# A sparse four-layer graph network on one core: two columns share one sum in the scan, and the first table is planned ahead of most of it

## The chip, the core and the metric

The kernel runs on one core of one Trainium2 chip. A core has five engines with instruction streams of their own: PE (TensorE, matmuls into PSUM), DVE (VectorE), ACT (ScalarE), POOL (GpSimd, which here issues the indirect DMAs) and SP (SyncE, which issues the plain DMAs). They meet at semaphores; transfers run on 16 DMA engines. The metric is the device time of one run in microseconds, less is better. The time before is 2148.46 us, the median of three runs (2143.64 to 2156.99).

## What is computed

Node features `x` (4096 x 256) go through four graph attention layers, each behind a layer norm, a ReLU and a residual. `adj` (4096 x 4096, int32) is 0 or 1, symmetric, with ones on the diagonal, and about 9 ones in a row.

```python
_a = jax.random.bernoulli(jax.random.fold_in(_gk, 2), 0.000976562, (4096, 4096))
_a = jnp.logical_or(_a, jnp.swapaxes(_a, -1, -2))
_a = jnp.logical_or(_a, jnp.eye(4096, dtype=bool))
adj = _a.astype(jnp.int32)
...
def _L0_gnn_ref(h, adj, W, a):
    Wh = (h @ W).reshape(n, heads, d)
    s_i = jnp.einsum('nhd,hd->nh', Wh, a[:, :d])
    s_j = jnp.einsum('nhd,hd->nh', Wh, a[:, d:])
    e = jax.nn.leaky_relu(s_i[:, None, :] + s_j[None, :, :], negative_slope=0.2)
    e = jnp.where((adj == 0)[:, :, None], -jnp.inf, e)
    alpha = jax.nn.softmax(e, axis=1)
    out = jnp.einsum('ijh,jhd->ihd', alpha, Wh).reshape(n, heads * d)
    return jax.nn.elu(out)
...
h = jnp.maximum(_layernorm(x, axis=-1), 0.0)
x = x + _L0_gnn_ref(h, adj, L0_gnn_W, L0_gnn_a)
```

Layers 1 to 3 have the same form with other score functions. Since a row has few neighbours, the kernel turns `adj` into lists of column numbers once and gathers only the neighbours' rows in every layer.

## The kernel before

The rows are 32 blocks of 128 ("rows" below: block r). The program has a first stage that makes the lists (`lists`, `scan`), then a re-reading of all rows in the order of their degrees (`reload`), the rest of layer 0 (`late`), layers 1 to 3 (`layer`), and a verdict. If a condition that the lists rely on does not hold (too many neighbours, for example), the verdict is bad and a dense version of the whole network runs behind it. Only the first stage is changed.

**The scan.** For every row block, four quarters of `adj` (128 x 1024 int32) come by DMA into eight buffers (`load`, L265) and ACT turns them into fp8 (`cast`, L276), which also sums the edges. `marks` (L491 to L498) handles 512 columns: one matmul multiplies the 0/1 columns with a diagonal matrix of MARK = 8192, a small one adds another MARK at the node's own column (so that it comes out first), and one adds each column's place, n minus its number. A PSUM value over 8192 is then an edge and says which; two MAX8 take the 8 largest of each 256 columns. Eight calls make a row block: 16 MAX8. `merge` (L506, L508) takes the 24 largest of these 128 candidates with three MAX8 and two replacements, and `number` (L514, L515, on ACT) turns them into column numbers.

**The table.** Beside it, for two row blocks at a time (`table`, u = 0 to 15), ACT applies norm and ReLU (L340), PE transposes (L348), ACT copies (L351), PE multiplies with the layer's weights (L892, fp32), and ACT copies the products to `s_keep` (L356); SP writes four row blocks at a time to a table in DRAM (L399). DVE's statistics for the norm are L580 and L581, its roots are L586 to L596.

**Early gathers.** `early(j)` handles row blocks 2j and 2j + 1: POOL fetches 6 neighbours of each of the 256 nodes with 12 indirect DMAs (L899, tile `s_g`, three buffers), DVE makes scores (L534 to L542), ACT the exponentials (L546), DVE the sums and the node's own term (L548, L550) and two multiplications of the gathered rows by their shares (L558, one per row block), PE adds the seven terms in fp32 (L564, L567), ACT copies the result (L571).

**Placing.** `sort` counts the degrees and finds each node's place (L607 to L650); `to_place` scatters a row block to that place with one indirect DMA (L656, 32 in all). `reload` waits for all of them.

**What sets the order.** PE, DVE, ACT and SP run in the order in which the program records the work. It is written by hand: a loop over steps `at` (four per 2048 columns, 256 in all for the scan) emits what `plan(engine, at, ...)` put there. In a step, ACT's and PE's planned work comes ahead of that step's marks, DVE's and POOL's behind them. Before, early gather j is fetched from step max(4(10 + j), 16(j + 1) + 3) on; its seven PE matmuls stand at every second step, the first on gathered rows four steps after the second multiplication; `sort` is planned 28 steps before the scan's end, and 12 of the 32 scatters may go out before it ends.

Of the kernel before, what the change touches and what calls it, by code (L numbers as in the profile page):

```python
# [9 lines left out]
F32 = mybir.dt.float32  # L10
# [38 lines left out]
MARK = 8192.0  # L49
# [30 lines left out]
class Sparse:  # L80
# [155 lines left out]
    def lists(self, w0, a0):  # L236
        tc, nc, nt, n = self.tc, self.nc, self.nt, self.n
        self.ok = self.const.tile([P, 8], F32, name="s_ok")
        nc.vector.memset(self.ok, 1.0)
        with ExitStack() as ctx:  # L240
            self.pool = ctx.enter_context(tc.tile_pool(name="s_scan", bufs=2))
            self.pacc = ctx.enter_context(tc.tile_pool(name="s_macc", bufs=4, space=PSUM))
            self.pp = ctx.enter_context(tc.tile_pool(name="s_mp", bufs=3, space=PSUM))
            self.pe = ctx.enter_context(tc.tile_pool(name="s_me", bufs=1, space=PSUM))
            self.top = self.pool.tile([P, nt, TOPK], F32, name="s_top", bufs=1)
            self.sums = self.pool.tile([P, nt, 4], F32, name="s_sums", bufs=1)

            self.keep = self.pool.tile([P, nt, ROW], F32, name="s_keep", bufs=1)
            self.ids = self.keep[:, :, OWN:].bitcast(U32)
            self.scan(w0, a0)  # L250

    def scan(self, w0, a0):
# [4 lines left out]
        halves, groups = 2 * nt, nt // 4  # L257
        raw, low = {}, {}
        state = {"load": 0, "cast": 0}

        def load(upto):
            while state["load"] < min(upto, 4 * nt):
                q = state["load"]
                raw[q] = self.pool.tile([P, n // 4], I32, name=f"s_raw_{q}", tag="raw", bufs=RAW)
                nc.sync.dma_start(  # L265
                    out=raw[q], in_=self.adj[ts(q // 4, P), ts(q % 4, n // 4)]
                )
                state["load"] += 1

        def cast(upto):  # L270
            while state["cast"] < min(upto, 4 * nt):
                q = state["cast"]
                r, h = divmod(q, 4)
                if h == 0:
                    low[r] = self.pool.tile([P, n], F8, name=f"s_low_{r}", tag="low", bufs=5)
                nc.scalar.activation(  # L276
                    low[r][:, ts(h, n // 4)], raw.pop(q), AF.Copy, saturate=False,
                    accum_out=self.sums[:, r, h : h + 1],
                )
                state["cast"] += 1  # L280

# [15 lines left out]
        def stats(g, k):  # L297
            if k == 0:
                norms[g] = self.norms_of(self.pool, xl(g), 4, f"t{g}")
            next(norms[g])  # L300
# [6 lines left out]
        next(first)  # L307
        self.tables()
        load(4)
        bring(1)  # L310
        load(RAW - 2)
        bring(2)
        self.constants()
        for g in range(3):
            for k in range(4):
                stats(g, k)
            next(norms[g])
            scaled(g)
            cast(2 * g + 2)
            if g == 0:  # L320
                *_, (self.we0, _) = first
        later = self.weights()
        next(later)
# [10 lines left out]
        def table(u):  # L334
# [9 lines left out]
            yield  # L344
# [7 lines left out]
            yield  # L352
            ps = [self.times(ht[:, k], self.we0, W, f"t0_{2 * u + k}") for k in range(2)]
            yield
            for k in range(2):
                nc.scalar.copy(self.keep[:, 2 * u + k, D : D + W], ps[k])  # L356
            yield

        for u in range(2 * groups):
            stages = table(u)  # L360
            step = lambda stages=stages: next(stages)
            for engine, after in (("act", 0), ("pe", 1), ("act", 2), ("pe", 4), ("act", 5)):
                plan(engine, 2 * u + after, step)
        for g in range(3, groups):
            begin = 4 * (g - 3)
            for k in range(4):
                plan("dve", begin + k, lambda g=g, k=k: stats(g, k))
            plan("act", begin + 6, lambda g=g: next(norms[g]))
            plan("dve", begin + 8, lambda g=g: scaled(g))
        for r in range(nt):  # L370
            plan("act", 8 * (r + 1) + 2, lambda r=r: self.number(r))
        whole, last = [], 0
        for j in range(nt // 2):
            begin = max(4 * (10 + j), 16 * (j + 1) + 3)
            stages = self.early(j)
            step = lambda stages=stages: next(stages)
            plan("pool", begin, step)

            last = max(last + 13 if j else begin + 24, begin + 17)
            plan("dve", last, step)  # L380
            for k in range(3):
                plan("dve", last + 2 + k, step)
            for k in range(EARLY + 1):
                plan("pe", last + 6 + 2 * k, step)
            plan("act", last + 2 * EARLY + 8, step)
            whole.append(last + 2 * EARLY + 8)
        counted = 4 * (halves - 7)
        sorting = self.sort()
        plan("pe", counted, lambda: next(sorting))
        plan("dve", counted + 1, lambda: next(sorting))  # L390
        placed = 0
        end = max(whole)
        for at in range(end + 1):
            t, s = divmod(at, 4)
            r, half = divmod(t, 2)
            if s == 0:
                g = t - 3
                if 0 <= g < groups:
                    nc.sync.dma_start(  # L399
                        out=self.tab[0][4 * g * P : 4 * (g + 1) * P, :].rearrange(  # L400
                            "(t p) w -> p t w", p=P
                        ),
                        in_=self.keep[:, 4 * g : 4 * (g + 1), D : D + W],
                    )
                if t + 3 < groups:
                    bring(t + 3)
                if 2 <= t < 7:
                    next(later, None)
            if s in (0, 2):
                load(state["cast"] + RAW)  # L410
                cast(2 * t + 4 + min(10, max(0, t - 8)) + s // 2 + 1)
            run("act", at)
            run("pe", at)
            if t < halves:
                if s == 0 and half == 0:
                    cand = self.pool.tile(
                        [P, n // CH, 8], F32, name=f"s_cand_{r}", tag="cand", bufs=2
                    )
                self.marks(r, 4 * half + s, low[r], cand)
                if s == 3 and half == 1:  # L420
                    self.merge(r, cand)
            run("dve", at)
            run("pool", at)
            if t > halves - 6 and not nt // 2 * 16 <= at < nt // 2 * 16 + 4:

                upto = min(placed + (2 if s % 2 else 1), 12 if t < halves else nt)
                while placed < upto and whole[placed // 2] < at:
# [7 lines left out]
    def constants(self):  # L435
# [4 lines left out]
        self.mark = const.tile([P, P], BF16, name="s_mark")  # L440
        nc.vector.tensor_scalar(self.mark, self.ident, MARK, None, ALU.mult)

        G = n // IB
# [16 lines left out]
            tall, pattern=[[-IB, G]], base=n - IB, channel_multiplier=0,  # L462
# [12 lines left out]
        nc.gpsimd.tensor_copy(self.ids[:, :, TOPK], own)  # L475

# [9 lines left out]
    def marks(self, r, g, lo, cand):  # L486
# [4 lines left out]
        nc.tensor.matmul(pt, lhsT=self.mark, rhs=lo[:, ts(g, IB)], start=True, stop=False)  # L491
        if g == r // SUB:
            nc.tensor.matmul(
                pt[:, ts(r % SUB, P)], lhsT=self.ident_bf, rhs=self.mark, start=False, stop=False
# [5 lines left out]
    def merge(self, r, cand):  # L500
# [3 lines left out]
        for k in range(TOPK // 8):  # L504
            m = self.top[:, r, ts(k, 8)]
# [4 lines left out]
    def number(self, r):  # L510

        nc, n = self.nc, self.n
        a = self.pool.tile([P, TOPK - 1], F32, name=f"s_ids_{r}", tag="ids")
        nc.scalar.activation(a, self.top[:, r, 1:], AF.Relu, bias=self.over)  # L514
        nc.scalar.activation(  # L515
            self.ids[:, r, 0 : TOPK - 1], a, AF.Relu, bias=self.none, scale=-1.0
        )

# [82 lines left out]
    def sort(self):  # L601
# [11 lines left out]
        num = lst.tile([P, Q], F32, name="s_num", bufs=1)  # L613
        nc.gpsimd.iota(
            num, pattern=[[-1, Q]], base=TOPK, channel_multiplier=0,
            allow_small_or_imprecise_dtypes=True,
        )
        unit = wide("s_unit")[:, : IB]
        nc.gpsimd.memset(unit, 1.0)
# [51 lines left out]
    def checks(self):  # L671

        nc, nt, ok, top, lst = self.nc, self.nt, self.ok, self.top, self.pool

        lim = lst.tile([P, TOPK], F32, name="s_lim", bufs=1)
        for q in range(TOPK):
            d = TOPK - 1 - q
            b = min([i for i, c in enumerate(CAPS) if c <= d] + [nt])
            nc.gpsimd.memset(lim[:, q : q + 1], float(P * b))
        over = lst.tile([P, TOPK], F32, name="s_over", bufs=1)  # L680
        nc.vector.tensor_tensor(over, self.ran[:, 0:TOPK, nt - 1], lim, ALU.is_le)
# [4 lines left out]
        nc.vector.tensor_scalar(some, top, MARK, None, ALU.is_gt)  # L686
        have = lst.tile([P, nt], F32, name="s_have", bufs=1)
        nc.vector.tensor_reduce(have, some, AX.X, ALU.add)
        nc.vector.tensor_tensor(have, have, self.edges, ALU.is_equal)
        nc.vector.tensor_reduce(ok[:, 0:1], have, AX.X, ALU.min)  # L690
        nc.vector.tensor_scalar(have, top[:, :, 0], 2.0 * MARK, None, ALU.is_gt)
        nc.vector.tensor_reduce(ok[:, 1:2], have, AX.X, ALU.min)
        nc.vector.tensor_scalar(have, top[:, :, 1], 2.0 * MARK, None, ALU.is_le)
        nc.vector.tensor_reduce(ok[:, 2:3], have, AX.X, ALU.min)
# [1286 lines left out]
```

## Time and profile before

| What | us |
|---|---|
| median of three runs | 2148.46 |
| span of the profiled execution, first to last instruction | 1756.1 |
| first early fetch on POOL | 96.3 |
| row block 31 numbered (L515) | 389.3 |
| last scatter to its place ends | 422.6 |
| first fetch of the rest of layer 0 | 427.1 |
| MAX8 of L498, 512 of them: sum of the group | 182.2 |
| POOL's early fetches, 192: sum of the group | 181.8 |

The page gives no time of the profiled execution other than its span. Slices are 43.9 us each, so the first stage is about slices 0 to 9. A row of the groups shows line, engine, operation, `out<-in`, count, busy time and mean, then the idle time just before the group and what ended it. In a timeline row the columns are start, duration, engine, line, operation, and in brackets the idle time before it with its releaser. An fp32 matmul shows as two PE records.

### The profile page before, as it was taken

To read this page: it belongs to the slowest core of one execution; us is meant where nothing else is said; L and a number is where in the kernel's file an instruction comes from. 1 tells how busy PE (TensorE), PEld (TensorE's weight loads), DVE (VectorE), ACT (ScalarE), POOL (GpSimd) and SP (SyncE) were. 2 spreads that over 40 slices of the span, in tenths; PEclk is the share of its full clock that TensorE was granted. 3 is DMA by queue.
4 is the path that set the end of the run, shared out by engine and by line. 5 is a ranking of instruction groups with operands and counts; after the bars stand their busy time and mean duration, and the time that the engine had idled before them with its cause. 6 is when DMAs were issued, how large, how long until landed. Compare 5 with 4: busy or idle time off the path is not lost. (4 is left out here: it accounts for less than half of the span.)

```text
span 1756.1 us, 13928 instructions
## 1 busy us (share of the span) xinstructions
PE 969.4 (55%) x2476; PEld 459.5 (26%) x2493; DVE 1355.2 (77%) x3733; ACT 427.0 (24%) x1222; POOL 1140.3 (65%) x1242
## 2 busy tenths in 40 slices
PE   4967777673467622222222177788775355455445
PEld 3622332221344411111111033344332122112112
DVE  6899889882668818888888367888876698888876
ACT  6875445200233401111111012222222000000000
POOL 1067655477477457777777477777773777777774
PEclk9989889886688855555555589889899677677787
DMA  9899878346733234444444244444543767776763
GB/s 328 280 379 368 289 268 292 108 144 216 220 104 109 70 89 126 133 131 131 133 130 131 72 114 132 136 134 132 139 132 107 216 200 212 209 210 192 209 203 110
DMA packets 121782, 309.05 MB, mean 176 GB/s; under 512 B 30900, under 2 KB 49335, under 8 KB 121688
## 3 DMA queue, kind: packets, MB, share of 16 engines
q0 software_dynamic: 66832, 203.64, 40.5%
q1 hardware_dynamic: 54856, 104.44, 16.9%
q14 instruction: 70, 0.57, 0.1%
q8 instruction: 24, 0.39, 0.1%
HBM read 272.99 MB, written 35.00 MB: 175 GB/s over the span
## 5 line engine op out<-in xcount | busy, mean ns | idle before, releaser
L899 POOL DMA_INDIRECT s_ring<-s_tab,s_near x900 | 854.7, 950 | 322.7 <-issue 179.1
L1354 PE MATMUL s_acc<-s_ring,s_ident 128*128 128x512 f32 x572 | 303.9, 683 | 112.2 <-issue 91.6
L899 POOL DMA_INDIRECT s_g<-s_tab,s_keep x192 | 181.8, 947 | 187.3 <-DMA s_raw<-in_adj_dram 90.4
L498 DVE MAX8 s_cand<-s_pt 128x8 f32<-128x256 f32 x512 | 182.2, 416 | 25.1 <-PE s_pt L496 24.1
L1354 PEld LDWEIGHTS s_acc<-s_ring,s_ident 128*128 128x128 f32 x572 | 123.5, 222 | 286.1 <-issue 228.1
L892 PE MATMUL s_ps<-s_we_l,s_ht 128*128 128x264 f32 x256 | 115.7, 608 | 80.1 <-ACT s_ht L1099 45.4
L1350 DVE TENSOR_TENSOR s_ring<-s_ring,s_shares 128x2048 f32<-128x2048 f32 (+7 forms) x94 | 154.8, 1673 | 0.0
L884 PE MATMUL s_pht<-s_ident,s_h 128*128 128x128 f32 x128 | 34.4, 361 | 202.9 <-ACT s_h L876 202.9
L567 PE MATMUL s_ae<-s_g,s_ident 128*128 128x512 f32 x192 | 116.5, 705 | 49.1 <-DVE s_g L558 48.7
L1322 DVE SCALAR_TENSOR_TENSOR s_acc<-s_ring,s_p,s_acc 128x256 f32<-128x256 f32 x269 | 131.8, 490 | 9.4
L276 ACT ACTIVATE s_low<-s_raw 128x1024 fp8e4<-128x1024 int32 x128 | 134.1, 1049 | 14.4 <-DMA s_raw<-in_adj_dram 14.2
L586 ACT ACTIVATE s_y<-s_mv,s_eps 128x1 f32<-128x1 f32 (+1 forms) x83 | 24.5, 295 | 408.9 <-DVE s_mv L581 408.9
L491 PE MATMUL s_pt<-s_low,s_mark 128*128 128x512 fp8e4 x256 | 107.5, 420 | 28.3 <-DVE s_cand L498 12.2
L892 PE MATMUL s_ps_kv<-s_wkv,s_ht 128*128 128x512 f32 x128 | 78.5, 745 | 67.5 <-ACT s_ht L886 67.5
L496 PE MATMUL s_pt<-s_places,s_stands 128*128 128x512 bf16 x239 | 99.1, 415 | 0.0
L892 PEld LDWEIGHTS s_ps<-s_we_l,s_ht 128*128 128x128 f32 x256 | 68.5, 290 | 110.6 <-ACT s_ht L1099 50.4
L1257 DVE TENSOR_TENSOR s_ring<-s_ring,s_shares 128x2048 f32<-128x2048 f32 (+7 forms) x47 | 78.8, 1676 | 21.1 <-DMA s_ring<-s_tab,s_near 21.1
L1279 ACT ACTIVATE s_shares<-s_e 128x40 f32<-128x40 f32 (+7 forms) x64 | 13.2, 206 | 327.0 <-DVE s_e L1272 317.0
L884 PEld LDWEIGHTS s_pht<-s_ident,s_h 128*128 128x128 f32 x128 | 18.0, 172 | 244.1 <-ACT s_h L876 232.7
L1260 DVE TENSOR_REDUCE s_e<-s_ring 128x32 f32<-128x2048 f32 (+7 forms) x47 | 78.9, 1679 | 1.6
L1343 PE MATMUL s_acc<-s_me,s_ident 128*128 128x512 f32 x60 | 39.3, 742 | 67.3 <-DVE s_me L1338 59.7
L1239 DVE TENSOR_TENSOR s_e<-s_ring,s_rx 128x9 f32<-128x9 f32 (+15 forms) x64 | 11.9, 187 | 79.0 <-DMA s_ring<-s_tab,s_near 74.9
(266 smaller groups left out, 1648.6 us busy)
## 6 DMA issues: line engine op xcount, KB each, us to landing
s_raw<-in_adj_dram SPq DMA_DIRECT2D x128, 512.0 KB, 7.4
s_ring<-s_tab,s_near POOLq DMA_INDIRECT x900, 2.9
s_rx<-s_placed SPq DMA_DIRECT2D x32, 262.0 KB, 7.0
s_tab<-s_kv SPq DMA_DIRECT2D x32, 256.0 KB, 2.8
s_tab<-s_keep SPq DMA_DIRECT2D x8, 528.0 KB, 6.8
s_tab<-s_rx SPq DMA_DIRECT2D x32, 132.0 KB, 1.9
s_keep<-in_x_dram SPq DMA_DIRECT2D x8, 512.0 KB, 8.8
s_vself<-s_tab SPq DMA_DIRECT2D x32, 128.0 KB, 2.9
```

Of the source, the lines that this page charges most:

```text
L276: nc.scalar.activation(low[r][:, ts(h, n // 4)], raw.pop(q), AF.Copy, saturate=False, accum_out=self.sums[:, r, h : h + 1],)
L491: nc.tensor.matmul(pt, lhsT=self.mark, rhs=lo[:, ts(g, IB)], start=True, stop=False)
L496: nc.tensor.matmul(pt, lhsT=self.stands[:, g, :], rhs=self.places, start=False, stop=True)
L498: nc.vector.max(out=cand[:, g * (IB // CH) + k, :], in_=pt[:, ts(k, CH)])
L567: nc.tensor.matmul(acc, lhsT=self.ident, rhs=g[:, :, k, 0:D], start=False, stop=(k == E - 1))
L892: self.nc.tensor.matmul(ps[:, :width], lhsT=ht[:, c, :], rhs=w[:, c, :], start=(c == 0), stop=(c == KC - 1),)
L899: return self.nc.gpsimd.indirect_dma_start(out=out, out_offset=None, in_=table[:, :], in_offset=bass.IndirectOffsetOnAxis(ap=idx, axis=0),)
L1257: nc.vector.tensor_tensor(kq, kq, q.unsqueeze(1).to_broadcast([P, m, D]), ALU.mult)
L1260: nc.vector.tensor_reduce(e[:, k0 : k0 + m, :], kq.rearrange("p k (h d) -> p k h d", h=4), AX.X, ALU.add)
L1322: nc.vector.scalar_tensor_tensor(acc, g[:, k, 0:D], p[:, k, :], acc, ALU.mult, ALU.add)
L1350: nc.vector.tensor_tensor(v, v, p[:, k0 : k0 + m, :].unsqueeze(3).to_broadcast([P, m, H, D // H]), ALU.mult)
L1354: nc.tensor.matmul(both, lhsT=self.ident, rhs=g[:, k : k + 2, v0 : v0 + D], start=(k == 0 and not full), stop=(k + 2 >= G and not more),)
```

## The change

Two columns 2048 apart now share one PSUM value: the lower one adds MARK + PAIR = 6144, the upper one MARK = 4096 (PAIR = 2048), and the place counts within 2048. A value of 4097 to 6144 is the upper column alone, 6145 to 8192 the lower alone, over 10240 both. `marks` has therefore four calls per row block, each with three full matmuls, and `merge` reads 64 candidates. The node's own edge is taken away instead of raised. `apart` splits the first value where it stands for both columns and shifts the list; one such pair per row is allowed for. Whether every node has its own edge is now read from the diagonal of `adj` by a DMA of its own (`own_edges`).

The scan has 128 steps. The table is recorded in the first nine, two stages ("ticks") per step; the loads of `x` stand at the very start. Early gather j is fetched at step 8j + 9, its DVE work stands at 8j + 20 to 8j + 23, its seven PE matmuls at 8j + 24 to 8j + 30, one per step. `sort` is recorded at steps 129 and 130, and no scatter ahead of the last fetch. `number` handles two row blocks at once. Some constants are made at the start instead of in `sort` and `checks`.

```diff
-MARK = 8192.0
+MARK = 4096.0
+PAIR = D * 8
...
+        quarter = lambda q: ts((0, 2, 1, 3)[q % 4], n // 4)
...
-                    low[r] = self.pool.tile([P, n], F8, name=f"s_low_{r}", tag="low", bufs=5)
+                    low[r] = self.pool.tile([P, n], F8, name=f"s_low_{r}", tag="low", bufs=4)
...
+                load(state["cast"] + RAW)
...
+        def tick(k):
+
+            g = k // 2 + 1
+            if k % 2 == 0 and g < groups:
+                roots(g)
+                scaled(g)
+            if k < 2 * groups:
+                made[k] = table(k)
+            for u in (k, k - 1, k - 2):
+                if u in made:
+                    next(made[u])
+            if k % 2 and g + 1 < groups:
+                stats(g + 1)
...
+            plan("act", 8 * j + 8, lambda j=j: self.number(j))
             stages = self.early(j)
             step = lambda stages=stages: next(stages)
-            plan("pool", begin, step)
-
-            last = max(last + 13 if j else begin + 24, begin + 17)
+            plan("pool", 8 * j + 9, step)
+            last = 8 * j + 20
             plan("dve", last, step)
             for k in range(3):
-                plan("dve", last + 2 + k, step)
+                plan("dve", last + 1 + k, step)
             for k in range(EARLY + 1):
-                plan("pe", last + 6 + 2 * k, step)
-            plan("act", last + 2 * EARLY + 8, step)
-            whole.append(last + 2 * EARLY + 8)
-        counted = 4 * (halves - 7)
+                plan("pe", last + 4 + k, step)
+            plan("act", last + EARLY + 5, step)
+            whole.append(last + EARLY + 5)
         sorting = self.sort()
-        plan("pe", counted, lambda: next(sorting))
-        plan("dve", counted + 1, lambda: next(sorting))
+        plan("pe", steps + 1, lambda: next(sorting))
+        plan("dve", steps + 2, lambda: next(sorting))
...
+            if at <= groups:
+                tick(2 * at)
+            if 2 <= at < 8:
+                next(later, None)
+            cast(at + 2 + min(10, at // 2))
             run("act", at)
             run("pe", at)
-            if t < halves:
+            if at < steps:
...
+                self.marks(r, g, low[r], cand)
+                if g == 3:
+                    self.merge(r, cand)
+                    if r % 2:
+                        self.apart(r // 2)
+            if at <= groups:
+                tick(2 * at + 1)
+            if at == steps // 2:
+                self.own_edges()
             run("dve", at)
             run("pool", at)
-            if t > halves - 6 and not nt // 2 * 16 <= at < nt // 2 * 16 + 4:
-
-                upto = min(placed + (2 if s % 2 else 1), 12 if t < halves else nt)
-                while placed < upto and whole[placed // 2] < at:
+            if at > 8 * (nt // 2 - 1) + 9:
+                while placed < nt and whole[placed // 2] < at:
...
-        nc.tensor.matmul(pt, lhsT=self.mark, rhs=lo[:, ts(g, IB)], start=True, stop=False)
-        if g == r // SUB:
+        for k in range(2):
             nc.tensor.matmul(
-                pt[:, ts(r % SUB, P)], lhsT=self.ident_bf, rhs=self.mark, start=False, stop=False
+                pt, lhsT=self.mark[k], rhs=lo[:, k * PAIR + g * IB : k * PAIR + (g + 1) * IB],
+                start=(k == 0), stop=False,
+            )
...
+    def apart(self, j):
+
+        nc = self.nc
+        top = self.top[:, 2 * j : 2 * j + 2, :]
+        to = self.found[:, 2 * j : 2 * j + 2, :]
+        two = self.pool.tile([P, 2, 1], F32, name=f"s_two_{j}", tag="two", bufs=2)
+        nc.vector.tensor_scalar(two, top[:, :, 1:2], 2.0 * MARK, None, ALU.is_gt)
+        nc.vector.tensor_scalar(top[:, :, 0:1], top[:, :, 1:2], -MARK, None, ALU.add)
+        nc.vector.scalar_tensor_tensor(
+            top[:, :, 1:2], two, -(MARK + PAIR), top[:, :, 1:2], ALU.mult, ALU.add
+        )
+        nc.vector.tensor_tensor(to, top[:, :, 0:TOPK], top[:, :, 1:], ALU.subtract)
+        nc.vector.tensor_tensor(to, to, two.to_broadcast([P, 2, TOPK]), ALU.mult)
+        nc.vector.tensor_tensor(to, to, top[:, :, 1:], ALU.add)
...
+    def own_edges(self):
+
+        nc, nt, n = self.nc, self.nt, self.n
+        self.loops = self.pool.tile([P, nt], I32, name="s_loops", bufs=1)
+        line = self.adj.rearrange("a b -> (a b)")[0 : n * n : n + 1]
+        with nc.allow_non_contiguous_dma(reason="the diagonal"):
+            nc.sync.dma_start(out=self.loops, in_=line.rearrange("(t p) -> p t", p=P))
```

## The prediction

> **What bounds the kernel now.** I read the page's busy shares and slices first, then the busy time by stage, then POOL, DVE and PE in order of time between 0 and 430 us. The page's chain of waits covers only the last 30 us of the span, so the scan's own chain is built from the timelines.
>
> ```profile
> DVE  6899889882668818888888367888876698888876
> POOL 1067655477477457777777477777773777777774
> 200.00:250.00 50.00, 38.10 (x115) 15.63 (x117) 46.86 (x134) 24.39 (x53) 30.80 (x33) 0.91 0.79 266
> 250.00:300.00 50.00, 41.37 (x123) 16.48 (x124) 44.21 (x130) 22.60 (x50) 27.48 (x30) 0.89 0.77 268
> 400.00:450.00 50.00, 10.81 (x25) 4.36 (x24) 15.56 (x50) 4.51 (x10) 35.32 (x41) 0.62 0.77 244
> ```
>
> The slices show DVE full until slice 9 (400 us), then a hole where only POOL works. The stage rows (PE, PEld, DVE, ACT, POOL busy, then clock, DMA share, GB/s) say the same: in 200 to 300 us DVE is busy 91 of 100, the DMA engines have a fifth to spare.
>
> ```profile
> 96.27 1.14 POOL L899 DMA_INDIRECT s_g<-s_tab,s_keep  x1 [90.45 <-DMA s_raw<-in_adj_dram]
> 395.78 0.94 POOL L899 DMA_INDIRECT s_g<-s_tab,s_keep  x1 [0.30 <-issue]
> 397.02 1.00 POOL L656 DMA_INDIRECT s_placed<-s_keep,s_pos  x1 [0.30 <-issue]
> 421.63 0.97 POOL L656 DMA_INDIRECT s_placed<-s_keep,s_pos  x1 [0.30 <-issue]
> ```
>
> This is POOL in order of time. The first fetch of neighbours waits until 96.27; the label names a raw load, but the last table write was issued at 87.79 and had to land. Row 31 is numbered at 389.3; then 6 fetches and 20 scatters follow back to back, and 421.63 + 0.97 = 422.6 us is the end of the stage. Everything after it (re-reading the rows, four layers) is untouched. So the change is worth what it does to 422.6.
>
> ```profile
> 283.67 1.73 DVE L558 TENSOR_TENSOR s_g<-s_g,s_pe 128x1536 f32<-128x1536 f32 x1
> 285.33 2.08 DVE L498 MAX8 s_cand<-s_pt 128x8 f32<-128x256 f32 x6
> 288.53 1.43 DVE L498 MAX8 s_cand<-s_pt 128x8 f32<-128x256 f32 x4 [1.13 <-PE s_pt L496]
> 285.46 2.07 PE L567 MATMUL s_ae<-s_g,s_ident 128*128 128x512 f32 x2 [2.60 <-DVE s_g L558]
> 287.33 0.63 PE L491 MATMUL s_pt<-s_low,s_mark 128*128 128x512 fp8e4 x1
> 288.92 1.02 PE L567 MATMUL s_ae<-s_g,s_ident 128*128 128x512 f32 x2
> ```
>
> And this is the hidden second limit. PE stood 2.60 us for the weighting (L558), came back at half clock (2.07 us for a float32 matmul, 1.02 once warm; pitches 1.86 and 0.86, marks 0.43 and 0.215), and DVE ran out of sums and waited 1.13.
>
> **Calibration.** In the steady part, two rows on DVE are: 32 MAX8 at 0.34 (eight in 2.73) = 10.9; two merges at 1.64 (269.77 to 271.41) = 3.3; one early gather 1.01 + 0.71 + 2 x 1.66 = 5.0. Sum 19.2. Walking PE beside it from the end of L558, with 4.1 us of half clock (I find 3.1 to 5.5 after seven such waits), adds 2.0 of waits: 21.2. Measured by the second fetch group of each pair (272.46, 293.90, 314.96, 337.41): 21.4, 21.1, 22.5. The method holds.
>
> **The change, DVE.** Per two rows 16 MAX8 go: -5.4. Merges read 64 instead of 128 candidates; from 256 elements (416 ns) to 128 (295 ns) is about 0.12, so 0.07 less on each of five instructions, 1.31 each: -0.7. The new apart has six instructions on 128x2 and 128x48; nearest rows are the chain L590/L591 (pitch 0.2) and L535 (0.20, pitch 0.23): 1.3, bounds 0.9 to 1.9. Left: 5.4 + 2.6 + 1.3 + 5.0 = 14.4.
>
> **The change, PE.** A step now has three marks matmuls instead of two and there are half as many steps: 24 per two rows instead of 32. But the seven matmuls of an early gather, one every second step before, now stand one per step, in seven of eight steps, and the first on gathered rows is one step earlier against its own weighting. Walk a period, t = 0 at the end of the second weighting (last step): PE has the sum of step 0 ready and is blocked. Step 1 needs one float32 matmul and three marks, cold: 0.1 + 1.86 + 0.86 + 0.63 = 3.45; DVE used 0.7 for step 0, so it waits 2.8. Step 2 ends at 5.4 (wait 1.3), step 3 at 7.0 (wait 0.85). Then the merge and the gather's DVE work put PE ahead. Steps 4 to 7: 9.1, 10.8, 12.2, 14.5, then 0.7 + 1.3 + 1.3 + 1.66 = 19.5. So 14.4 becomes 19.4 to 19.5: of 6.1 us taken from DVE, 1.3 go to apart and 3 return as waits for PE. PE finishes step 0 of the next period near t = 14 and stands about 6 us, so it is cold again each time.
>
> [...] In the trace 2.60 us was enough. [...]
>
> **The change, start.** The table now runs in nine steps, and the first fetch waits for all of it. One step is a loop: ACT relu and two copies 2.0, transposes 0.45, eight f32 passes 1.78, marks 0.85, two MAX8 0.68, then the statistics of a later group, 2.35, for which the next step's root on ACT waits: 8.2 us. (ACT's own sum per step is 6.1.) First root waiting on x group 1: DVE 8.5 (as now) + 1.25 + 3.6 + 2.4 = 15.9. Step 0 at half clock 8.5, steps 1 to 5 41.0 and a merge 1.3, then ACT-bound 5.6 + 5.1 + 4.4: 82 for the last table write; + 8.5 to the first fetch as now = 90. Bounds 80 to 100 (loop 6.1 to 9.6). On SP the writes of x and the table stand ahead of raw loads; eight raw buffers cover it.
>
> Twelve fetches at 1.25 and 5.7 to land: scores of pair 0 at 110, and DVE, which by then has done the scan steps to 20 at 5 us a row, stands for about 12 us. That stall exists only because the gather is planned 12 steps after its fetch.
>
> **The sum.** 110, + 9.7 to the end of that period, + 13 x 19.5 = 373.2; the last apart ends 1.7 before it, numbering on ACT 0.8 and the issue 0.2: last fetch group at 372.5. Now 389.3 was its place, so the scan gains 17. But in the built order all 32 scatters stand behind the 16th fetch group, and both rows of the last pair are fetched together: 12 x 1.25 + 32 x 1.277 = 55.9 instead of 33.4. The sort, moved behind the scan, takes 11.5 (338.9 to 350.5) beside 15 us of fetches: hidden, and if late, by 1 or 2 us. End 428.4.
>
> The diagonal load (4096 elements of 4 bytes) goes into SP's queue at step 64, ahead of raw loads. Nearest: 428 to 438 us, 3798 packets under 512 B among 2.86 MB at 286 GB/s, where 110 to 150 us ran 394: at most 2.7 us for all engines. ACT casts up to ten quarters ahead, so I take 1; bounds 0 to 10, no gain possible. POOL's memsets for limits already ran before 6 us: nothing. The checks' DVE work (3 us at 404) stays under the scatters.
>
> 422.6 becomes 429.4: +7. The page gives the profiled execution's span, 1756.1, and not its whole time; the median of the runs, 2148.46, is 392.4 above the span, in no view, and I keep it. 2148.5 + 7 = 2155.
>
> **Rivals.**
> A, faster (0.14): PE stays warm or has more lead than I give it. Warm, the waits are 2.7 and the period 17.1: 31 us less, 2124. With no wait for PE the floor is POOL's 12 x 1.25 = 15 per pair: 58 less, 2097. For it: PE's sum is only 11.4 of 19.5 at full clock. Against it: all seven restarts in the trace are cold, and the calibration needed the waits.
> B, slower (0.27): the half clock outlasts the PE-bound steps 1 to 3. All three cold, step 3 ends at 9.8, the period at 22.2: +35, 2190. It decides against the kernel from a period of 20.6 on, a half clock of about 6.5 us. [...] Against: the longest seen is 5.5.
> C, no effect (0.58): as summed, own range 2135 to 2171.
> D, the sums cannot be told apart in some row and the dense branch runs, milliseconds more (0.01): counted in the reference's own draw, 39 rows have one pair of neighbours 2048 apart, none has two, and no 256 sums hold more than 7.
>
> **How the numbers follow.** 1% is 21.5 us, about what a measurement can tell from no change. Faster by more: A but for its mild cases, 0.15. Slower by more: B and D, 0.28. Between: 0.57. The unknowns (apart 6, clock 8, start 8, diagonal 5 us, as halves of their spans over 13 periods) give about +/- 14 by themselves; reaching to A's warm case and B's end leaves 2 in 10 out: 2120 to 2190.
>
> **What would show it.** Right: fetches start near 90, DVE's waits for PE at the marks grow from 25 to 60 us or more, pairs come every 19.5 us, POOL runs 44 DMAs without a gap from about 372 to 428. Wrong: pairs under 17.5 us or restarts at full clock (A); pairs over 20.6 (B); raw loads as the releaser of casts in mid-scan (the diagonal or the DMA engines, which I left out); a first fetch after 100.

## The result, and the profile after

| | before | after |
|---|---|---|
| median of 20 runs each, us | 2149.47 (2140.78 to 2162.73) | 2155.30 (2146.84 to 2165.79) |
| ratio to before | | 1.003, 95% interval 1.0015 to 1.0044 |

The change costs about 6 us, within 1%. But the span of after's profile, 2157.4 us, is nearly its time, whereas before's was 392 us short of it. Second profiles of both kernels (`e0_before`, `e0_after` below) and a third of before (`e2_before`) settle what the shown one of before was. On two chips every run of before takes 1756 to 1761 us, on two others its medians are 2127 to 2145 (2149 in the 20 runs), with instructions of the same duration (a MAX8 in the rows below: 420 and 421 ns) but pauses between them (the last section has rows); the shown profile of before is of the first kind, its timed runs and the profile of after are of the second. Whether it is the chip itself or something else that differed there isn't shown; "kind of chip" below means no more than this. Compared kind by kind (each column one profiled execution, us):

| | before, as shown | after (`e0_after`) | before (`e2_before`) | after |
|---|---|---|---|---|
| span | 1756.1 | 1774.5 | 2126.4 | 2157.4 |
| first early fetch | 96.3 | 97.0 | 96.8 | 97.0 |
| last scatter ends | 422.6 | 438.4 | 480.7 | 492.5 |
| first fetch of the rest of layer 0 to the end | 1329.0 | 1331.3 | 1640.2 | 1660.2 |

The last row is work that the change doesn't touch: on chips of the first kind it takes 1327 to 1332 us in all seven profiles of this study, on the others 1640 to 1660 from one profile to the next. The stage that is changed got longer by 15.8 us on the first kind of chip and by 11.8 on the second. (On the first kind there are two profiles of each kernel: the stage ends at 422.6 and 422.9 before, at 438.4 and 440.9 after.)

The row of the MAX8, first from the page of after (second kind of chip), then from that of `e0_after` (first kind), and the stage rows of `e0_after` (PE, PEld, DVE, ACT, POOL busy, clock, DMA share, GB/s):

```profile
L527 DVE MAX8 s_cand<-s_pt 128x8 f32<-128x256 f32 x256 | 96.2, 420 | 140.5 <-PE s_pt L525 82.5
```

```profile
L527 DVE MAX8 s_cand<-s_pt 128x8 f32<-128x256 f32 x256 | 96.3, 421 | 98.9 <-PE s_pt L525 98.9
```

```profile
200.00:250.00 50.00, 33.68 (x93) 13.73 (x93) 34.61 (x111) 26.14 (x55) 27.39 (x29) 0.83 0.93 299
250.00:300.00 50.00, 37.91 (x110) 15.08 (x108) 36.58 (x117) 23.53 (x49) 29.32 (x31) 0.86 0.87 292
```

DVE, 91 of 100 busy before in 200 to 300 us, is busy 71 of 100 on the same kind of chip (58 in after's own profile): half of the MAX8 are gone (512 of 182 us in sum became 256 of 96), and DVE now stands in front of the remaining ones for 98.9 us, and for 140.5 where pauses are added. POOL, in order of time, in `e0_after`, on the kind of chip that the prediction was worked out from:

```profile
96.95 1.14 POOL L945 DMA_INDIRECT s_g<-s_tab,s_keep  x1 [91.30 <-ACT s_low L277]
144.75 0.94 POOL L945 DMA_INDIRECT s_g<-s_tab,s_keep  x1 [2.88 <-ACT s_keep L561]
...
362.43 0.94 POOL L945 DMA_INDIRECT s_g<-s_tab,s_keep  x1 [4.90 <-ACT s_keep L561]
382.47 0.94 POOL L945 DMA_INDIRECT s_g<-s_tab,s_keep  x1 [5.34 <-ACT s_keep L561]
397.53 1.01 POOL L706 DMA_INDIRECT s_placed<-s_keep,s_pos  x1 [0.30 <-DVE s_ee L588]
...
437.42 0.97 POOL L706 DMA_INDIRECT s_placed<-s_keep,s_pos  x1 [0.30 <-issue]
```

The first fetch is at 97 again; then eleven periods of two row blocks take 362.43 - 144.75 = 217.7, 19.8 each; the last fetch group starts at 382.5, only 7 us before the place where row 31 used to be numbered, and all 32 scatters stand behind it: 437.42 + 0.97 = 438.4. Where a period of 19.8 goes on DVE:

```profile
244.39 0.76 DVE L527 MAX8 s_cand<-s_pt 128x8 f32<-128x256 f32 x2
247.92 0.77 DVE L527 MAX8 s_cand<-s_pt 128x8 f32<-128x256 f32 x2 [2.77 <-PE s_pt L525]
250.12 0.77 DVE L527 MAX8 s_cand<-s_pt 128x8 f32<-128x256 f32 x2 [1.44 <-PE s_pt L525]
251.62 0.77 DVE L527 MAX8 s_cand<-s_pt 128x8 f32<-128x256 f32 x2 [0.74 <-PE s_pt L525]
```

and on PE beside it:

```profile
244.52 2.08 PE L621 MATMUL s_ae<-s_g,s_ident 128*128 128x512 f32 x2 [5.33 <-DVE s_g L612]
...
249.92 1.02 PE L621 MATMUL s_ae<-s_g,s_ident 128*128 128x512 f32 x2
```

PE stood 5.33 us for the second weighting, came back at half clock (2.08 instead of 1.02), and the first three sums of the period came late: 2.77, 1.44 and 0.74 us of waiting, then none. The granted clock stands in the profile too. PE in `e0_after` by stretches whose edges are set where the clock changes (length, busy, clock as a share of full speed, DMA share, GB/s):

```profile
242.32:249.15 6.83, 4.63 (x7) 0.50 0.95 317
249.15:262.80 13.65, 9.43 (x33) 1.00 0.85 285
324.24:327.65 3.41, 2.84 (x5) 0.50 0.84 247
```

The half clock began at 242.32, while PE stood, and lasted until 249.15: 4.6 us of work at half clock from the restart at 244.52. In the whole stage of this profile DVE waits 98.9 us for PE at the marks, against 24.1 in the shown profile of before. Of these, 66.5 us stand behind 95 us, in the scan (20.9 before), and some 32 ahead of it, in the loop that makes the table (some 3 before).

### The profile page after: what moved, and what is told of

It is laid out like the page before. It is cut to its first block, busy times and chain, and to the rows that moved or that the text cites. A ratio compares the mean times of both kernels' runs of the same rounds, so it can differ in the third digit from the quotient of the medians.

```text
span 2157.4 us, 13417 instructions
## 1 busy us (share of the span) xinstructions
PE 957.0 (44%) x2350; PEld 457.6 (21%) x2365; DVE 1279.5 (59%) x3577; ACT 418.6 (19%) x1190; POOL 1141.3 (53%) x1241
## 5 line engine op out<-in xcount | busy, mean ns | idle before, releaser
L1400 PE MATMUL s_acc<-s_ring,s_ident 128*128 128x512 f32 x572 | 308.4, 691 | 143.0 <-issue 116.6
L527 DVE MAX8 s_cand<-s_pt 128x8 f32<-128x256 f32 x256 | 96.2, 420 | 140.5 <-PE s_pt L525 82.5
L938 PE MATMUL s_ps_kv<-s_wkv,s_ht 128*128 128x512 f32 x128 | 91.9, 858 | 112.3 <-ACT s_ht L932 46.6
L1303 DVE TENSOR_TENSOR s_ring<-s_ring,s_shares 128x2048 f32<-128x2048 f32 (+7 forms) x47 | 78.8, 1676 | 17.9 <-DMA s_ring<-s_tab,s_near 17.4
L515 PE MATMUL s_pt<-s_low,s_mark_True 128*128 128x512 fp8e4 x256 | 85.8, 418 | 3.4 <-DVE s_cand L527 1.9
L955 POOL DMA_INDIRECT s_tab<-s_rx,s_near x32 | 32.1, 1002 | 82.1 <-ACT s_rx L1154 37.2
L621 PEld LDWEIGHTS s_ae<-s_g,s_ident 128*128 128x128 f32 x192 | 42.6, 232 | 149.4 <-DVE s_g L612 131.4
```

Source lines behind the costliest of these rows:

```text
L515: nc.tensor.matmul(pt, lhsT=self.mark[k], rhs=lo[:, k * PAIR + g * IB : k * PAIR + (g + 1) * IB], start=(k == 0), stop=False,)
L527: nc.vector.max(out=cand[:, g * (IB // CH) + k, :], in_=pt[:, ts(k, CH)])
L621: nc.tensor.matmul(acc, lhsT=self.ident, rhs=g[:, :, k, 0:D], start=False, stop=(k == E - 1))
L938: self.nc.tensor.matmul(ps[:, :width], lhsT=ht[:, c, :], rhs=w[:, c, :], start=(c == 0), stop=(c == KC - 1),)
L1303: nc.vector.tensor_tensor(kq, kq, q.unsqueeze(1).to_broadcast([P, m, D]), ALU.mult)
L1400: nc.tensor.matmul(both, lhsT=self.ident, rhs=g[:, k : k + 2, v0 : v0 + D], start=(k == 0 and not full), stop=(k + 2 >= G and not more),)
```

## The experiments

Each variant is one edit of the changed kernel unless said otherwise. Ratios are to the kernel before on the same chip.

**`e0_before` and `e0_after`: what did the shown profile of before stand for?** No edit.

> The kernel before, unchanged, for a second profile of it. Theory 1, the shown profile of before (span 1756.1 us) is one execution that does not stand for the timed runs (2141 to 2163 us): this profile has a span near 2147 us, its first stage ends near 485 us instead of 422.6, and the stages that the change does not touch take about 1660 us as in the profile of after (1665), not 1333. Theory 2, some 392 us lie outside the span in every execution of before: the span is again near 1756 us, the stage ends near 423 us, and the change has then made the untouched stages 330 us longer.

> The changed kernel, unchanged, for a second profile on the same chip. Theory 1: span near 2153 us, first stage ends near 490 us, periods of two rows near 23.4 us, as in its first profile. Theory 2: the same, since nothing is said about this kernel.

Before took 1758.9 us (span 1757.2), after 1776.3 (span 1774.5), on one chip. Each theory was half wrong: the span is again 1757 us, but so is the time, so the shown profile is a normal one, of a chip of the first kind, and nothing lies outside the span; what had been added in the prediction as 392 us outside it is spread over the whole program on other chips. Of after, both theories expected 490 and 23.4 again; it showed 438.4 and 19.8.

**`e1_after`: the change timed on a chip of the first kind.** No edit.

> The changed kernel, unchanged, timed in rounds with the kernel before and with the three variants on one chip. Theory 1: 15 to 18 us more than the kernel before, as in the one look on a chip where the kernel before takes 1759 us; or 3 to 9 us more where the kernel before takes 2149 us. Theory 2, the one look was scatter: 3 to 9 us more on either kind of chip.

1773.1 against 1757.5 us, ratio 1.0088 (1.0071 to 1.0105): 15.6 us. So the cost of the change there is real and larger than on the chip of the 20 runs, where it is 1.003 (to 1.0044).

**`e2_before`: before on a chip of the second kind.** No edit.

> The kernel before, unchanged, once more, for a profile of it where it takes about 2149 us, as in the timed runs of the result; its earlier profiles are of executions of 1757 us. Theory 1, on such a chip engines stand for stretches without a cause in the program, and the kernel with more instructions there loses more: the stage up to the last scatter ends 55 to 70 us later than 422, near 480 to 490, and after's 492.6 is 3 to 13 us more. Theory 2, the stage is not touched and the later stages lose it all: the stage ends near 425. Where the chip gives 1757 us again, the run says nothing on this.

2128.1 us, and the first theory's number was met:

```profile
479.70 0.97 POOL L656 DMA_INDIRECT s_placed<-s_keep,s_pos  x1 [0.30 <-issue]
```

This is the last scatter of before there. The stage ends at 480.7, 58.1 later than in its shown profile; after's ends 54.1 later than in `e0_after`. The two kernels lose about the same in this stage.

**`x1_lead`: more lead for the early matmuls.** This tests the step on which the prediction rests, that DVE's waits come from PE being sent to wait for the weighting.

```diff
-                plan("pe", last + 4 + k, step)
-            plan("act", last + EARLY + 5, step)
-            whole.append(last + EARLY + 5)
+                plan("pe", last + 7 + k, step)
+            plan("act", last + EARLY + 8, step)
+            whole.append(last + EARLY + 8)
```

> The changed kernel with the early gather's seven PE matmuls three steps later against the weighting. Theory 1, the prediction's: of a period of two rows DVE has 14.4 us of work and some 5 us of waits for PE, which was sent to wait for the weighting and came back cold; with the lead DVE's waits at the marks fall from 99 us to under 25, the period falls from 19.8 to the 15.0 us of POOL's 12 fetches, the first fetch stays at 97, the last fetch group starts near 325 instead of 382, the stage ends near 382 instead of 438, so 50 to 58 us less than the changed kernel. Rival: the loads of adj are the next bound (DMA share 0.94 and 0.90 between 100 and 300 us in the second profile of the changed kernel): then casts wait for raw loads, the period is 17.5 or more, and the gain is at most 30 us.

1715.9 us, ratio 0.9759 (0.9741 to 0.9777): 57.2 less than the changed kernel and 41.6 less than before. POOL and the stage rows of this variant (columns as above):

```profile
97.02 1.14 POOL L945 DMA_INDIRECT s_g<-s_tab,s_keep  x1 [91.34 <-DMA s_raw<-in_adj_dram]
...
378.26 0.97 POOL L706 DMA_INDIRECT s_placed<-s_keep,s_pos  x1 [0.30 <-issue]
```

```profile
100.00:200.00 100.00, 71.34 (x224) 29.86 (x222) 79.77 (x265) 62.41 (x129) 75.62 (x81) 0.85 1.03 394
200.00:300.00 100.00, 81.17 (x262) 34.02 (x261) 92.21 (x299) 64.95 (x132) 75.84 (x80) 0.95 0.99 359
```

From 97.02 to 378.26 POOL never stands more than 0.4 us ahead of a DMA: it is now the bound, and a period is its 15.0 us. What DVE waits for PE at the marks (us, times, longest):

```profile
DVE s_cand L527 <- PE s_pt L525: 32.1, 9, 5.5
```

All nine of these waits stand ahead of 95 us, in the loop of the table, which this edit doesn't touch; in the scan the 66.5 us are gone altogether. (The 25 expected was below what the loop alone takes.) The rival saw something true, the DMA engines at 1.03 and 0.99, but casts waited only 7.9 us for raw loads.

**`x2_warm`: no stand, so no cold clock.** 22 bf16 matmuls with zero weights fill the stand ahead of the first gathered matmul.

```diff
         yield
+        flat = acc.rearrange("p u d -> p (u d)")
+        for k in range(WARM):
+            nc.tensor.matmul(flat, lhsT=self.zero, rhs=self.places, start=False, stop=False)
         for k in range(E):
```

> The changed kernel with 22 bf16 matmuls of zero weights (about 0.21 us each at full clock, 4.7 us) ahead of the first matmul on gathered rows, so that PE works instead of standing for 5 to 6 us. Theory 1, the prediction's: half clock after that stand costs each period 2.2 us of DVE waits (4.95 cold, 2.7 warm); the first fp32 matmul after the stand takes 1.02 instead of 2.08 us, the waits at the marks fall from 99 to about 60 us, the period from 19.8 to 17.5, and the time is 26 to 34 us less than the changed kernel. Rival, the order of the work on PE alone makes the waits and the clock does not matter: waits and period stay within 0.5 us of the changed kernel's, or grow where the added work is in the way.

1743.6 us, ratio 0.9924 (0.9907 to 0.9941): 29.4 less than the changed kernel, by adding work. PE's order of time:

```profile
242.73 2.75 PE L625 MATMUL s_ae<-s_places,s_zero 128*128 128x512 bf16 x12
246.13 1.12 PE L627 MATMUL s_ae<-s_g,s_ident 128*128 128x512 f32 x2 [0.64 <-DVE s_g L615]
```

After a stand of 0.64 instead of 5.33 us the first matmul takes 1.12 instead of 2.08, DVE's waits for PE fall from 99 to 65.5 (in the scan from 66.5 to 37.3), and twelve periods are 17.3 to 17.4 us each. The granted clock is 1.00 from 121.4 to 360.4 us. A warm clock alone thus gives half of what the lead gives; the other half of the scan's waits comes from the order of the work on PE.

**`x3_tail` and `x7_tail`: the sort inside the scan again, some scatters ahead of the last fetch.**

```diff
-        plan("pe", steps + 1, lambda: next(sorting))
-        plan("dve", steps + 2, lambda: next(sorting))
+        plan("pe", steps - 10, lambda: next(sorting))
+        plan("dve", steps - 9, lambda: next(sorting))
...
-            if at > 8 * (nt // 2 - 1) + 9:
-                while placed < nt and whole[placed // 2] < at:
+            if at > steps - 9:
+                upto = min(placed + 1, 9) if at <= 8 * (nt // 2 - 1) + 9 else nt
+                while placed < upto and whole[placed // 2] < at:
```

> The changed kernel with the sort 11 steps earlier, inside the scan, and nine scatters ahead of the last fetch group. Theory 1: the tail of 55.9 us behind the last group shrinks by 9 x 1.277 = 11.5, but the sort's 11.5 us on DVE now stand in the scan and POOL is pressed in the last period: the time is within 5 us of the changed kernel's. Rival, the 32 scatters behind the last fetch are plain loss: 9 to 12 us less.

A miss: 1781.0 us, 7.9 more than the changed kernel (ratio 1.0132, 1.0115 to 1.0149). POOL shows why:

```profile
372.41 1.00 POOL L707 DMA_INDIRECT s_placed<-s_keep,s_pos  x1 [15.28 <-DVE s_pos L701]
373.72 0.97 POOL L946 DMA_INDIRECT s_g<-s_tab,s_keep  x1 [0.30 <-issue]
```

One scatter came out ahead of the 15th fetch group, and on POOL, which runs in order, that group stood behind it until the sort was done. `x7_tail` starts the scatters one step later (`at > steps - 8`), behind that group.

> The earlier sort again, with the first scatter now behind the 15th fetch group and eight scatters ahead of the 16th, so that no fetch stands behind a scatter that waits for the sort. Theory 1: the 8 x 1.277 = 10.2 us less of tail are paid back by the sort's 11.5 us of DVE work inside the scan, which delays the last numbers by 6 to 11 us: within 5 us of the changed kernel's place against the kernel before (ratio 1.006 to 1.011 where the kernel before takes 1757 us, 1.001 to 1.006 where it takes 2149). Rival, the scatters behind the last fetch are plain loss: 9 to 12 us less than the changed kernel (ratio 1.002 to 1.004, or 0.997 to 0.999).

It ran on a chip of the second kind: 2137.6 against 2131.5 us, ratio 1.0033 (1.0016 to 1.005), which is the changed kernel's 1.003. So on that kind of chip eight scatters fewer behind the last fetch gain nothing that the timing shows; a few us either way can't be told from it. The theory's reason isn't shown: in its profile the last fetch group was numbered at 425.5 and stood until 431.7 behind the eight scatters, and the stage ended at 484.9, ahead of after's 492.5. On the first kind it wasn't tried in this form.

**`x4_nodiag`: without the load of the diagonal.**

```diff
-            nc.sync.dma_start(out=self.loops, in_=line.rearrange("(t p) -> p t", p=P))
+        nc.gpsimd.memset(self.loops, 1)
```

> The changed kernel without the load of adj's diagonal; ones are written instead, so whether every node has its own edge is not tested. Theory 1, the prediction's: the 4096 elements of 4 bytes cost 1 us of the time, since casts run up to ten quarters ahead: within 3 us of the changed kernel. Rival, the upper bound: it holds up raw loads and casts, 10 us less.

2156.4 against 2145.1 us, ratio 1.0048 (1.0032 to 1.0065), no less than the changed kernel's 1.003 (on another chip). A cost of 10 us (0.5%) is excluded on this kind of chip; 1 us is below what this shows.

**`x5_stats`: the statistics ahead of the sums in the table loop.**

```diff
                 roots(g)
                 scaled(g)
+                if g + 1 < groups:
+                    stats(g + 1)
...
-            if k % 2 and g + 1 < groups:
-                stats(g + 1)
```

> The changed kernel with the statistics of the next group recorded ahead of a step's sums instead of behind them. Theory 1: a step of the table loop takes 9.8 us because ACT's root waits for statistics, these stand on DVE behind MAX8, MAX8 waits for PE, and PE for ACT's copies; without that ring ACT's own 6.1 to 6.6 us remain, the last table write goes from 90 to 62 to 70, the first fetch from 97 to 70 to 80, and the time is 15 to 27 us less than the changed kernel's. Rival: the loads (x, first quarters of adj, weights) or PE set the step: the first fetch stays above 90 and the gain is under 7 us.

2134.8 us, ratio 0.9951 (0.993 to 0.9972), against 1.003 of the changed kernel: 0.8%, 17 us. SP's table writes of this variant and its first fetch:

```profile
52.02 0.38 SPq L365 DMA_DIRECT2D s_tab<-s_keep  x1
58.56 0.38 SPq L365 DMA_DIRECT2D s_tab<-s_keep  x1
...
69.58 0.38 SPq L365 DMA_DIRECT2D s_tab<-s_keep  x1
```

```profile
78.20 1.13 POOL L945 DMA_INDIRECT s_g<-s_tab,s_keep  x1 [72.56 <-DMA s_raw<-in_adj_dram]
```

The last write went from 90.2 to 69.6. From the second write to the seventh a step takes 5.9 us in the mean (34.48 to 63.96), in `e0_after` 9.3 (38.13 to 84.58); the last step takes 5.6 in both. The first theory holds, and the fetch comes 14 to 20 us earlier (92 to 98 in the other profiles without this edit). With the ring of waits the half clock went as well: the granted clock is 1.00 from 24 to 78.5 us, where `e0_after` has 3.41 us of half clock in each of five steps. The run doesn't part the two.

**`x6_both` and `e2_both`: lead and statistics together, run twice.**

> The later matmuls of the lead variant (57 us less than the changed kernel) and the earlier statistics together. Theory 1: POOL issues without a gap from the first fetch to the last scatter in the lead variant, so what the start gains comes out at the end: 15 to 27 us less than the lead variant, about 1695 us where the kernel before takes 1757. Rival: in the lead variant the DMA engines are full between 100 and 300 us (shares 1.03 and 0.99), so the loads of adj hold the scan back: at most 8 us less than the lead variant.

> The lead and the earlier statistics together, once more on another chip. Theory 1: POOL's chain from the first fetch sets the end; 75 to 84 us less than the changed kernel and 60 to 70 less than the kernel before on a chip where that takes 1757 us, as on the one of 2145 us, where it was 64 less. Rival, the loads of adj hold it back where instructions run faster: at most 50 us less than the kernel before, as little as the lead alone (42) or less.

2081.0 against 2145.1 us (ratio 0.9702, 0.9674 to 0.9729) and 2073.5 against 2127.4 (0.9727, 0.9683 to 0.977): 64 and 54 us less than before, so this version beats both kernels. Both runs fell on one and the same chip, of the second kind, where POOL isn't gapless (it stands 3 to 7 us between most groups, for the numbers), so whether the start's gain comes out whole at the end of a gapless POOL, and whether the DMA engines stop it, could not be read: on the first kind of chip this version wasn't run.

## Why the prediction was right, and what in it was not

The time came out as said (2155.3 against 2155), and so did the mechanism of the scan. That it came out to the microsecond is luck: two terms of the sum were off, and their errors cancel in the total.

**What bounds it.** Right. DVE gave way to waits for PE, and to nothing else: with the lead (`x1_lead`) the scan's waits go, and 57 us with them, where rival A had put 58 for no wait at all; with a warm PE (`x2_warm`) 29 us go, where it had put 31.

**Walk of a period.** Waits of 2.8, 1.3 and 0.85 at steps 1 to 3 were predicted; the rows show 2.77, 1.44 and 0.74, and over twelve periods the means are 2.8, 1.7 and 0.8. The period was to be 19.5 and is 19.8, and 17.35 warm, where 17.1 was said. Two small errors partly cancel in it. The apart chain, taken at 1.3, takes 1.06 (261.22 to 262.28 in `e0_after`). And the half clock was taken at 4.1 us, which is what the clock of before shows behind its stands of 2.6 to 4.4 us; behind the longer stands of `e0_after`, 5.3 to 5.4 us, it lasts 2.8 to 6.2 us from the restart, 5.0 in the mean of the twelve. That mean would have been the better value: a matmul takes 2.08 at half clock and 1.02 warm in `e0_after`, so 0.9 us more of half clock adds about 0.45 to the walk's 19.5, and less the 0.24 of the apart that is 19.7 (an estimate from these numbers). Two readings there were loose as well: the first gathered matmul moved two steps closer to its weighting, from four to two, not one; and not all seven restarts in before were cold throughout (the first pair takes 1.41 us at 212.87, and in `e0_before` 1.13 at 178.07 after 2.60 us of standing).

**Start.** This term failed. The loop of the table was summed to 8.2 us a step and the first fetch to 90; measured are 9.8 and 97.0. PE and ACT rows of one such step in `e0_after`:

```profile
59.59 1.95 PE L938 MATMUL s_ps_t<-s_we_l,s_ht_t 128*128 128x264 f32 x8
64.32 0.67 PE L355 MATMUL s_pt_t<-s_ident,s_h_t 128*128 128x128 f32 x4 [2.78 <-ACT s_ht_t L358]
64.81 3.63 PE L938 MATMUL s_ps_t<-s_we_l,s_ht_t 128*128 128x264 f32 x8
```

```profile
72.05 0.30 ACT L640 ACTIVATE s_y_t<-s_mv_t,s_eps 128x4 f32<-128x4 f32 x1 [3.19 <-DVE s_mv_t L635]
```

The eight fp32 passes were taken at 1.78 us, from their start to that of the next work. One set in two takes that (1.95 in its row, to the end of its last pass), but the one that the loop waits for comes after PE stood 2.78 us for ACT: its row is 3.63, and the next work starts 3.47 after it (at 68.28). These 1.7 us are the whole excess of a step, 9.8 against 8.2: the half clock, which the prediction counted in the scan, was left out of the loop, whose ring of waits it had right (ACT for statistics, these behind MAX8, MAX8 for PE).

**Last fetch group and tail.** 372.5 was said, 382.5 measured: 7 from the start, the rest from the 13 longer periods. The tail of 55.9 is 438.4 - 382.5 = 55.9, gapless. That the sort is hidden behind the fetches holds (POOL goes from fetch to scatter in 0.30), and the time of `x7_tail` shows no gain from moving it back.

**The diagonal.** 1 us: not contradicted, and not resolved.

**The sum.** +7 was said; on the chips that the profile was of, the stage is +15.8 and the time +15.6 (`e1_after`), the start being the term that was too small. On the chip of the 20 runs it is +5.8 between medians. The step that failed there is the assumption that the 392 us between the span and the median lie outside the program and stay as they are. They lie inside it (in `e2_before` 58 us in the first stage and 311 behind it), and what they add differs between the kernels. So the time was met to a microsecond by 8.6 us of cost that was left out, most of it at the start, and some 10 us of a difference between chips that the prediction knew nothing of. Why after loses some 10 us less than before on that chip is open. It isn't so on every chip of that kind: on the chip of `x4_nodiag` and `e2_before` the change without the diagonal cost 11.3 us, and its stage ended 11.1 later. That after has 511 instructions fewer (13417 against 13928) fits, if each of them costs its share of the pauses (392 / 13928 = 0.03 us each, 14 us for 511), but no run tests it.

**The rivals.** A's two prices were right, but it needed other edits. B, with a half clock of 6.5 us that outlasts step 3, isn't seen, though the longest from a restart, 6.2 us, comes near. D did not happen.

**What would show it.** Waits of 60 us or more: 98.9, of which the scan's 66.5 are those that the walk made (thirteen times 4.95 is 64) and the table loop's 32 were not foreseen. 44 DMAs without a gap: yes. Pairs every 19.5: 19.8. Fetches near 90: no. In the profile of after alone, the list would have misled: its period of 23.4 is over the 20.6 that was to prove B, and its cause isn't the clock (half for 3.1 to 6.2 us from a restart there, no longer than in `e0_after`) but the pauses between instructions (41.2 us before its MAX8 with "remote" and "issue" as releasers, none in `e0_after`).

## What to carry to other kernels

When an engine is relieved, look at how far ahead of its producer each consumer's work is recorded on the next engine: a quarter of a period's work left DVE here (19.2 us by the prediction's sum became 14.4), and most of the gain went into waits because seven matmuls stood too close behind a weighting; moving them three steps was worth 57 us, where the change itself had cost 16. PE, when it stood 2.8 or 5.4 us here, paid twice, in the stand and in the half clock after it (2.08 for 1.02 us in the scan, 3.63 for 1.95 in the table's loop), so count the clock in every loop that makes PE wait, the prologue's too. And where a profile's span isn't the time of the timed runs, as here with 1756 against 2148, take another profile before adding the difference as a constant.

## What the runs showed of the hardware

**Pauses on the second kind of chip.** The instructions compared have the same durations on both kinds (MAX8 420 ns in after, 421 in `e0_after`; a weighting, L612, 1.75 us in both), but on the second there are stretches in which DVE starts an instruction only every 0.7 or 1.4 us (from 560 to 960 us, 37 pairs of DVE starts lie 1.4 apart in after and 37 in `e2_before`, none in `e0_after`). Two stretches of one line of layer 1, DVE in order of time, first in after, then in `e0_after`:

```profile
814.53 0.49 DVE L1368 SCALAR_TENSOR_TENSOR s_acc<-s_ring,s_p,s_acc 128x256 f32<-128x256 f32 x1 [0.90 <-DVE s_acc L1368]
815.93 0.49 DVE L1368 SCALAR_TENSOR_TENSOR s_acc<-s_ring,s_p,s_acc 128x256 f32<-128x256 f32 x1 [0.91 <-DVE s_acc L1368]
```

```profile
739.50 6.26 DVE L1368 SCALAR_TENSOR_TENSOR s_acc<-s_ring,s_p,s_acc 128x256 f32<-128x256 f32 x12
```

12 of them in 6.26 us are 0.52 each, against 1.40. Inside the scan pauses stand in most periods, and the releaser that the profile names can be a chance one:

```profile
307.62 0.67 DVE L604 TENSOR_TENSOR s_mee<-s_keep,s_pe 128x512 f32<-128x512 f32 x1
310.45 0.76 DVE L527 MAX8 s_cand<-s_pt 128x8 f32<-128x256 f32 x2 [2.16 <-PE s_pt L525]
```

These are DVE rows of after. The sum that the last of them reads was finished on PE at 306.3, and DVE was free at 308.3; the matmul that ended as it started belongs to a later sum. In `e0_after` there is no such wait at this place. The cause of the pauses isn't settled by these runs; "remote" and "issue" as releasers (29.6 and 11.6 us before MAX8 in 95 to 430 us of after, none in `e0_after`) are their mark.

**A period that beats against the clock's grid.** In `e0_after` the granted clock changes only on a grid of 3.41 us, and from 126 to 368 us its half-clock stretches are 3.41 or 6.83 us long: 242.32 to 249.15 and 324.24 to 327.65 in the rows shown. There the periods are 19.65, 20.07, 20.28, 20.37, 18.69, then 19.56, 20.07, 20.28, 20.37, 18.74 us: the pattern repeats after five, 99.06 and 99.02 us. The granted clock of before and of after changes on such a grid too: the half clock from 414.96 to 466.17 us in before, 51.2 us, is 15 steps of 3.413, and 29 such steps are 98.98 us. With PE kept warm the pattern is gone (12 periods of 17.3 to 17.4). The short stretch goes with the short period: where the clock came back 2.8 us after the restart, the period was 18.7, where it took 6.1, it was 20.4. So in this trace the half clock lasted 2.8 to 6.2 us from a restart, depending on where the stand fell on the grid, and a sum over these periods comes nearest with the mean, 5.0. A stand shorter than one step of the grid was followed by it too: in before the first matmul after 2.60 us took 2.08 at 176.33, but after the same 2.60 us 1.13 at 178.07 in `e0_before`.
